# A gated scan followed by a conditioned GRU: direct products of x in the first steps, steps laced into the last chunk, and a first gate in blocks

## The chip, the cores and the metric

The kernel runs on one core of a Trainium2 chip. The core has a matrix engine (PE, with its weight loads shown apart as PEld), a vector engine (DVE), an activation engine (ACT), a general engine (POOL) and a queue engine (SP); each works through its own instructions in order and they wait for each other by semaphores. Transfers are issued from a queue (mostly SP's) and run beside the engines. The metric is the device time of one execution in microseconds (us); lower is better. A profiled execution leaves a record of every instruction, from which the views in this document are taken.

## What is computed

Two layers over x of shape (64 batches, 128 tokens, 512 features), all in 32-bit floats. Layer 0 is a gated linear recurrence that can be done by scans; layer 1 is a GRU whose steps follow each other. Cut to what matters:

```
# layer 0, on x; h0 = cond (64 x 512)
f, i  = sigmoid(x W_f^T + b_f), sigmoid(x W_i^T + b_i)
fn,in = f / (f + i + eps), i / (f + i + eps)
new   = in * (x W_h^T + b_h)
L     = cumsum(log(fn + eps))                 # over tokens
hid   = cumsum(exp(L[-1] - L[t-1]) * new) + exp(L) * h0
x     = x + hid
# layer 1, on the new x; v = cond C + b for each of the gates r, z, h
for t in range(128):                          # h starts at zero
    z  = sigmoid(x_t W_z + h U_z + v_z)
    r  = sigmoid(x_t W_r + h U_r + v_r)
    hh = tanh(x_t W + (r * h) U + v_h)
    h  = (1 - z) * h + z * hh
    out_t = x_t + h
```

## The kernel before

**Layer 0.** The batches go in 16 groups `g` of 4 (`GB`), that is 512 columns of (token, batch). x is loaded with tokens on the partitions, in four blocks of 128 columns per group, and transposed on PE (`x_transposed`, through the helper `transposed`, whose matmuls are L144 and whose copy out of PSUM is L145). The features go in four chunks `c` of 128. For each chunk `chunk_products` makes three gates on PE (`gate`, L181: four 128x512 products each), with the sigmoids of the first two on ACT (L222, L226). Then DVE does the chunk: the sum of both gates (L243), its reciprocal (L244), two products (L258, L261), with ACT adding eps between (L260), then `chunk_new` (L268, a scan L269), `chunk_retained` (a scan backwards L276, a product L281) and `chunk_initial` (a scan L286). POOL works beside the next chunk's reciprocal: the start values (L248), `sums` (L215) and `add_hidden` (L197), which adds x and stores the new x to a DRAM tile `x2d`. `tie` adds an ordering wait, so that these POOL instructions begin after L243. In group 0 the weights of layer 0 have to be transposed too (`w0_transposed`), and behind group 0 `conditioning` computes v on PE (L318).

**Layer 1.** The batches form two streams of 32, so that one stream's products run while the other waits for its sigmoid. In `Stream.step`, a step is: on PE 16 products of h for the gates r and z (L348, g, 256 columns), on ACT the sigmoid (L540), on DVE r times h (L542) and its transpose (L543), on PE 16 products for the candidate (128 columns), on ACT tanh (L570), on DVE the update (L574, L580) and the transpose of the new h (L587). The sum that PE adds to lies in PSUM (`g0` and `g1`, one for each stream) and begins with a share that ACT copies there (`put_share`, L517). A product with zeros comes once before the first share in each.

The share of x is made for two steps at a time by Winograd's form of Strassen's scheme: `queue_pair` puts 7 block products into a list, as 14 units of 4 matmuls (192 columns); they need `s4`, four sums of x on POOL (`gather`, L461 to L464, after an ACT copy L454), and are read out by additions on DVE (L482) and POOL (L485). `fill(n)` issues n units, 7 in each step, between the two products of h, where PE would wait for the sigmoid. The additions are issued in the steps behind (`read`). v is stored as its first half and the difference of its halves, as the additions need it.

**The passage.** Stream 0 needs batches 0 to 31 only, so its gathers 0 and 1 can be made before layer 0 ends. In the last chunk (g = 15, c = 3) the order is written out by hand: `chunk_norm`, gather 1, all of pair 0 and read out, step 0 with pair 1 in it, `chunk_new`, step 1 with `chunk_retained` inside, `chunk_initial`; then the last new x for the first 16 tokens and stream 1's gather 0, its pair 0, read out, and the loop over t from `LEAD` = 2, which alternates stream 0's step t and stream 1's step t - 2. Stream 0's steps 126 and 127 and the end of stream 1 have too few units left to fill; stream 1's steps 126 and 127 are alone, and there `idle_products` multiplies zeros.

`pin` keeps instructions in the program's order on their engine.

Of the kernel before, what the change touches and what calls it, by code (L numbers as in the profile page):

```python
# [14 lines left out]
P = 128  # L15
# [3 lines left out]
def kernel(  # L19
# [72 lines left out]
    def load_x(g, tb, tag="x", bufs=2, queue=nc.sync):  # L92
        rows = work.tile([P, D], F32, tag=tag, bufs=bufs, name=f"x_{g}_{tb}")
        queue.dma_start(
            rows,
            x[g * GB : (g + 1) * GB, tb * TB : (tb + 1) * TB, :].rearrange("b t d -> t b d"),
        )
        x_rows[g, tb] = rows

    load_w_rows(0, 0)  # L100
    for tb in range(K):
        load_x(0, tb, tag="h", bufs=5, queue=(nc.sync, nc.scalar)[tb % 2])
    bias0 = const.tile([3 * K, P], F32, name="bias0")
    for n, v in enumerate((b_f, b_i, b_h)):
        nc.sync.dma_start(bias0[n * K : (n + 1) * K, :], v.rearrange("(c p) -> c p", p=P))
# [63 lines left out]
    w0_transposed(0, 0)  # L169
    for tb in range(K):  # L170
        x_transposed(0, tb, copy=(nc.vector.tensor_copy, nc.scalar.copy)[tb % 2])
# [3 lines left out]
    transposed(biasT, bias0, n=3 * K, m=1)  # L175

    def gate(g, c, n):
        p = psum.tile([P, NT], F32, tag=f"p{n}", name=f"p{n}_{g}_{c}")
        for k in range(K):
            pin(  # L180
                nc.tensor.matmul(  # L181
                    p,
                    lhsT=W0[:, c, n, k, :],
                    rhs=xT[g][:, k, :],
                    start=(k == 0),
                    stop=(k == K - 1),
                )
            )
# [28 lines left out]
    def chunk_products(g, c):  # L217
# [5 lines left out]
        if g == 0 and c == 0:  # L223
            w0_transposed(c, 1)
        p = gate(g, c, 1)
        pin(nc.scalar.activation(ib, p, AF.Sigmoid, bias=biasT[:, 0, K + c : K + c + 1]))  # L226
        if g == 0 and c == 0:
            w0_transposed(c, 2)
            transposed(condT, cond_sb, n=B)
        if g == 0 and c + 1 < K:  # L230
            for n in range(3):
                w0_transposed(c + 1, n)
# [3 lines left out]
        return gate(g, c, 2)  # L236

    def chunk_norm(g, c):
# [14 lines left out]
        if g > 0 or c > 0:  # L253
            before = (g, c - 1) if c else (g - 1, K - 1)
            beside += [sums(*before), add_hidden(*before)]
        for instruction in beside:
            tie(instruction, total)
        pin(nc.vector.tensor_tensor(f, f, h, ALU.mult))  # L258
        fb = by_batch(f)
        pin(nc.scalar.activation(fb, fb, AF.Copy, bias=EPS))  # L260
        return pin(nc.vector.tensor_tensor(i, i, h, ALU.mult))  # L261
# [39 lines left out]
    def conditioning():  # L301
# [27 lines left out]
        for s in range(2):  # L329
            v = const.tile([P, 2, 3, HP], F32, name=f"v{s}")  # L330
            halves, bias_ = (t.rearrange("p g (n e) -> p n g e", n=2) for t in (ps[s], bias1))
            pin(nc.vector.tensor_tensor(v, halves, bias_, ALU.add))
            pin(nc.vector.tensor_tensor(v[:, 1], v[:, 1], v[:, 0], ALU.subtract))
            vs.append(v)
# [56 lines left out]
    def fill(n):  # L391
        for _ in range(n):
            if to_fill:
                unit, reads = to_fill.pop(0)
                unit()
                to_read.extend(reads)
# [12 lines left out]
    class Stream:  # L409
        def __init__(self, s):  # L410
            self.s = s
            self.v = vs[s]
            self.batches = slice(s * SB, (s + 1) * SB)
            self.h = None
# [4 lines left out]
            self.hT = zeros  # L419
# [28 lines left out]
        def gather(self, n):  # L448

# [11 lines left out]
            first_sum = pin(nc.gpsimd.tensor_tensor(s1, a21, a22, ALU.add))  # L461
            pin(nc.gpsimd.tensor_tensor(s2, s1, a11, ALU.subtract))
            pin(nc.gpsimd.tensor_tensor(s3, a11, a21, ALU.subtract))
            pin(nc.gpsimd.tensor_tensor(s4_, a12, s2, ALU.subtract))  # L464
            return first_sum
# [53 lines left out]
        def step(self, t, n_fill=7, n_idle=0, between=None):  # L519
# [4 lines left out]
            xz = self.xz[t // 2 % 2][:, t % 2]  # L524
# [8 lines left out]
            if t > 0:  # L533
# [13 lines left out]
            else:  # L547
                matmuls(g, lambda k: hT_, [w_s[:, 0]], stop=False)
                pin(nc.scalar.activation(rz, xz[:, RZ], AF.Sigmoid))
            fill(n_fill)  # L550
            idle_products(n_idle)
# [167 lines left out]
```

## Time and profile before

| | |
|---|---|
| three runs, median (lowest to highest) | 1995.42 us (1995.08 to 1996.5) |
| the profiled execution: its own time | 1994.23 us |
| its span, first to last instruction | 1992.5 us |
| mean granted TensorE clock | 0.996 |
| PE busy | 1962.2 us, 98% |
| PE weight loads | 1502.6 us, 75% |
| DVE busy | 1367.5 us, 69% |
| POOL busy | 756.0 us, 38% |
| ACT busy | 483.6 us, 24% |
| chain that ended last | PE 66%, DVE 32%, issue 1%, ACT 1% |

How to read it: 98% busy for PE is an average over stages with different limits, and the ends of matmuls are modelled, so a busy PE is not PE at its peak. What a change in one stage is worth is read in that stage. The chain of waits is followed back from the last instruction: at each step to what released it, or to the instruction before it on its engine. In a group row such as "PE g L348 x64" the count is of records; each fp32 matmul leaves two, so x64 is 32 matmuls. Times inside the span are us from its start.

### The profile page before, as it was taken

How to read it: one execution, taken by the hardware profiler on the slowest of the kernel's cores; microseconds unless marked ns; L12 is line 12 of the kernel's file. 1: busy time of each engine (PE TensorE's matmuls, PEld its weight loads, DVE VectorE, ACT ScalarE, POOL GpSimd, SP SyncE). 2: the span in 40 equal slices, each digit the busy share in tenths (PEclk: the TensorE clock that was granted, in tenths of full speed). 3: DMA queues.
4: the chain of work that ended last, by engine and by line, in shares of the span. 5: the costliest groups of instructions: out<-in, count | busy, mean ns of one | idle time of the engine just before them, and what ended most of it. 6: DMA issues, size and time to landing. Idle time of an engine off the chain costs nothing.

```text
span 1992.5 us, 73938 instructions
## 1 busy us (share of the span) xinstructions
PE 1962.2 (98%) x32809; PEld 1502.6 (75%) x32809; DVE 1367.5 (69%) x3017; ACT 483.6 (24%) x1104; POOL 756.0 (38%) x1482
## 2 busy tenths in 40 slices
PE   8999999999999979999999999999999999999997
PEld 4544444444444447777799999999999999999996
DVE  5899999999999975555555555555555555555554
ACT  3222212122122212222222222222222222222222
POOL 1222222222223234444444444444444444444442
PEclk9999999999999989999999999999999999999999
DMA  5411111211111211300220211121120121100111
GB/s 177 170 56 48 48 43 53 63 58 53 43 48 48 71 33 24 62 14 15 43 36 14 40 37 17 35 40 19 35 40 14 19 56 19 20 14 14 19 19 19
DMA packets 228408, 84.66 MB, mean 42 GB/s; under 512 B 205484, under 2 KB 205496, under 8 KB 228088
## 3 DMA queue, kind: packets, MB, share of 16 engines
q1 hardware_dynamic: 227224, 79.34, 16.1%
q8 instruction: 258, 4.23, 0.9%
q10 hardware_dynamic: 864, 0.59, 0.1%
q14 instruction: 62, 0.51, 0.1%
HBM read 46.34 MB, written 33.55 MB: 40 GB/s over the span
## 4 chain that ended last, share of the span: by engine, by line
PE 66%; DVE 32%; issue 1%; ACT 1%; DMA 0%; DVEq 0%; POOL 0%; ACTq 0%; SPq 0%; POOLq 0%
PE g L348 33%; PE m L348 29%; DVE h L244 10%; DVE h L286 4%; DVE i L269 4%; DVE h L276 3%; PE p L181 2%; DVE i L268 2%; DVE i L281 2%; DVE f L258 2%; DVE i L261 2%; DVE h L243 2%; PE tp L144 0%; PE pv L318 0%; DMA x<-in_x_dram 0%
## 5 line engine op out<-in xcount | busy, mean ns | idle before, releaser
L181 PE MATMUL p<-xT,W 128*128 128x512 f32 x1536 | 667.6, 592 | 1.4 <-ACT W L145 0.9
L181 PEld LDWEIGHTS p<-xT,W 128*128 128x128 f32 x1536 | 287.9, 190 | 345.9 <-issue 339.1
L348 PE MATMUL g<-w_s,h 128*32 128x256 f32 x8128 | 503.0, 380 | 2.1 <-DVE h L587 2.1
L348 PEld LDWEIGHTS g<-w_s,h 128*32 128x32 f32 x8128 | 374.7, 110 | 35.3 <-ACT g L517 2.7
L348 PE MATMUL m<-w_t,s 128*32 128x192 f32 x6144 | 345.2, 327 | 0.0
L574 DVE TENSOR_TENSOR h<-h,f 128x128 f32<-128x128 f32 x254 | 74.2, 292 | 343.6 <-ACT h L570 343.6
L589 POOL TENSOR_TENSOR o<-o,h 128x128 f32<-128x128 f32 x254 | 116.3, 458 | 462.4 <-DVE h L580 461.9
L348 PE MATMUL g<-w_s,f 128*32 128x128 f32 x8128 | 285.1, 273 | 4.6 <-DVE f L543 4.5
L348 PEld LDWEIGHTS m<-w_t,s 128*32 128x32 f32 x6144 | 256.3, 110 | 18.2
L348 PEld LDWEIGHTS g<-w_s,f 128*32 128x32 f32 x8128 | 254.2, 110 | 11.3 <-ACT f L540 5.5
L570 ACT ACTIVATE h<-g 128x128 f32<-128x128 f32 x254 | 70.4, 277 | 698.5 <-PE g L348 698.5
L482 DVE TENSOR_TENSOR W<-m,W 128x192 f32<-128x192 f32 x640 | 207.3, 339 | 20.5 <-PE m L348 2.7
L244 DVE RECIPROCAL h<-h 128x517 f32<-128x517 f32 x64 | 217.0, 3391 | 2.2
L248 POOL COPY first<-condT 128x4 f32<-128x4 f32 x64 | 12.1, 190 | 521.0 <-DVE h L243 502.6
L348 PE MATMUL m<-w_x,x 128*32 128x192 f32 x4096 | 200.0, 328 | 6.6 <-ACT x L454 6.6
L542 DVE TENSOR_TENSOR f<-f,h 128x128 f32<-128x128 f32 x254 | 86.3, 340 | 153.3 <-ACT f L540 153.3
L348 PEld LDWEIGHTS m<-w_x,x 128*32 128x32 f32 x4096 | 167.6, 111 | 22.1 <-ACT x L454 6.8
L545 POOL TENSOR_SCALAR f<-f 128x128 f32<-128x128 f32 x254 | 75.5, 297 | 204.8 <-DVE f L542 204.8
L260 ACT ACTIVATE f<-f 128x512 f32<-128x512 f32 x64 | 40.3, 630 | 459.1 <-DVE f L258 459.1
L485 POOL TENSOR_TENSOR W<-W 128x192 f32<-128x192 f32 x256 | 148.0, 600 | 4.8 <-DVE W L482 4.8
L540 ACT ACTIVATE f<-g 128x256 f32<-128x256 f32 x254 | 97.4, 384 | 214.1 <-PE g L348 211.7
L517 ACT COPY g<-W 128x384 f32<-128x384 f32 x254 | 122.7, 483 | 19.2 <-ACT h L570 1.1
(77 smaller groups left out, 1960.3 us busy)
## 6 DMA issues: line engine op xcount, KB each, us to landing
x2d<-x SPq DMA_DIRECT2D x63, 256.0 KB, 2.0
x<-in_x_dram SPq DMA_DIRECT2D x62, 256.0 KB, 3.0
out_dram<-o SPq DMA_DIRECT2D x248, 64.0 KB, 2.0
xw<-x2d SPq DMA_DIRECT2D x60, 256.0 KB, 4.6
w_rows<-in_L_cond_W_f_dram SPq DMA_DIRECT2D x4, 256.0 KB, 3.9
w_rows<-in_L_cond_W_i_dram SPq DMA_DIRECT2D x4, 256.0 KB, 4.0
w_rows<-in_L_cond_W_h_dram SPq DMA_DIRECT2D x4, 256.0 KB, 5.0
w_s<-in_L_cond_U_r_dram SPq DMA_DIRECT2D x1, 1024.0 KB, 5.8
```

The costliest lines, as they stand in the source:

```text
L181: nc.tensor.matmul(p, lhsT=W0[:, c, n, k, :], rhs=xT[g][:, k, :], start=(k == 0), stop=(k == K - 1),)
L244: pin(nc.vector.reciprocal(h, h))
L269: pin(nc.vector.tensor_tensor_scan(i, i, f, 0.0, ALU.add, ALU.mult))
L286: pin(nc.vector.tensor_tensor_scan(h, fs[c % 2], first, 0.0, ALU.mult, ALU.add))
L348: nc.tensor.matmul(p[q * SB : (q + 1) * SB], lhsT=lhsT(k), rhs=part(wk, q), start=(start and k == 0), stop=(stop and k == len(w) - 1), ski ...
L482: return lambda: pin(nc.vector.tensor_tensor(dst, p, other, ALU.add))
L485: return lambda: pin(nc.gpsimd.tensor_tensor(dst, a, b_, ALU.add))
L517: pin(nc.scalar.copy(self.g, self.xz[t // 2 % 2][:, t % 2]))
L540: pin(nc.scalar.activation(rz, g[:, RZ], AF.Sigmoid))
L542: pin(nc.vector.tensor_tensor(rh, r, h_, ALU.mult))
L545: pin(nc.gpsimd.tensor_scalar(r, z, -1.0, 1.0, ALU.mult, ALU.add))
L589: pin(nc.gpsimd.tensor_tensor(o, o, h, ALU.add))
```

## The change

Six steps (0 to 3 of stream 0, 0 and 1 of stream 1) no longer get their share of x from the pairs. ACT copies v whole into the PSUM place (`put_v`), and PE adds the products of x onto it directly, 16 matmuls of 384 columns (`x_products`). The pairs 0 and 1 of stream 0 and 0 of stream 1, and so their additions, are gone. Stream 0 uses both PSUM places at its start, g0 for step 0 and g1 for step 1. Step 0 now stands before the last chunk's `chunk_norm`, step 1 inside it (between the reciprocal and the products with it on DVE in part), step 2 around `chunk_retained`. Gather 0 of stream 0 is made one group earlier, and the four sums of its gather 1 go one by one to the POOL work of four chunks (`spare`). At the end the last pair of stream 1 is queued earlier, and from t = 125 on four units fill a step instead of seven; zeros fill in where no units are left.

In group 0 the first gate is computed in four blocks of 128 columns, each after its block of x, all x blocks come on SP's queue and the biases on ACT's, and each weight's transposes stand one gate ahead of its use, instead of all three behind the second gate.

```
@@ loads
-    def load_x(g, tb, tag="x", bufs=2, queue=nc.sync):
+    def load_x(g, tb, tag="x", bufs=2):
...
-        load_x(0, tb, tag="h", bufs=5, queue=(nc.sync, nc.scalar)[tb % 2])
+        load_x(0, tb, tag="h", bufs=5)
...
-        nc.sync.dma_start(bias0[n * K : (n + 1) * K, :], v.rearrange("(c p) -> c p", p=P))
+        nc.scalar.dma_start(bias0[n * K : (n + 1) * K, :], v.rearrange("(c p) -> c p", p=P))
@@ gate
-    w0_transposed(0, 0)
-    for tb in range(K):
-        x_transposed(0, tb, copy=(nc.vector.tensor_copy, nc.scalar.copy)[tb % 2])
...
-    transposed(biasT, bias0, n=3 * K, m=1)
...
+        blocks = [slice(0, NT)]
+        if (g, c, n) == (0, 0, 0):
+            copies = (nc.vector.tensor_copy, nc.scalar.copy)
+            blocks = [slice(tb * P, (tb + 1) * P) for tb in range(K)]
+            w0_transposed(0, 0)
+            for tb in range(2):
+                x_transposed(0, tb, copy=copies[tb % 2])
+        for tb, tokens in enumerate(blocks):
+            for k in range(K):
+                pin(nc.tensor.matmul(p[:, tokens], lhsT=W0[:, c, n, k, :],
+                    rhs=xT[g][:, k, tokens], start=(k == 0), stop=(k == K - 1)))
+            if len(blocks) > 1 and tb + 2 < K:
+                x_transposed(0, tb + 2, copy=copies[tb % 2])
+            elif len(blocks) > 1 and tb + 2 == K:
+                transposed(biasT, bias0, n=3 * K, m=1)
+                w0_transposed(0, 1)
@@ chunk_products (group 0)
         if g == 0 and c == 0:
-            w0_transposed(c, 1)
+            w0_transposed(0, 2)
+        elif g == 0 and c + 1 < K:
+            w0_transposed(c + 1, 0)
...
-            w0_transposed(c, 2)
             transposed(condT, cond_sb, n=B)
-        if g == 0 and c + 1 < K:
-            for n in range(3):
-                w0_transposed(c + 1, n)
+            w0_transposed(1, 0)
+        elif g == 0 and c + 1 < K:
+            w0_transposed(c + 1, 1)
...
+        if g == 0 and c + 1 < K:
+            for n in range(1 if c == 0 else 2, 3):
+                w0_transposed(c + 1, n)
@@ chunk_norm
+        if spare:
+            beside.append(spare.pop(0)())
...
+        if between:
+            between(normed)
+        else:
+            normed()
@@ Stream
+        def put_v(self):
+            pin(nc.scalar.copy(self.g, self.whole_v))
+
+        def x_products(self, t):
+            x_ = self.x4[t // 4 % 2][:, t % 4]
+            matmuls(self.g, lambda k: x_[:, k * SB : (k + 1) * SB],
+                [w_x[:, k] for k in range(K)], start=False, stop=False)
@@ the passage
-    tie(st0.gather(1), normed)
-    st0.queue_pair(0)
-    fill(2 * 7)
-    read_all()
-    st0.queue_pair(1)
-    st0.step(0, n_fill=2 * 7)
+    g0, g1 = st0.g, st1.g
+    for place in (g0, g1):
+        matmuls(place, lambda _: zeros, [w_s[:, 0]], stop=False)
+        st0.g = place
+        st0.put_v()
+        st0.x_products(0 if place is g0 else 1)
+    st0.g = g0
+    st0.step(0, n_fill=0, share=False)
+    st0.put_v()
+    def x_of_step_2():
+        st0.g = g0
+        st0.x_products(2)
+        st0.g = g1
+    def step_1(rest):
+        st0.g = g1
+        st0.step(1, n_fill=0, share=False, filler=x_of_step_2, between=rest)
+        st0.g = g0
+    chunk_norm(g, c, between=step_1)
+    st1.put_v()
     chunk_new(g, c, p)
     st0.queue_pair(2)
-    st0.step(1, between=lambda: chunk_retained(g, c))
+    fill(7)
+    st0.step(2, share=False, between=lambda: chunk_retained(g, c))
+    st0.put_v()
+    st0.x_products(3)
     chunk_initial(g, c)
...
-    later = to_fill[:]
-    to_fill.clear()
-    st1.queue_pair(0)
-    fill(2 * 7)
-    read_all()
-    to_fill.extend(later)
+    st1.x_products(0)
     for t in range(LEAD, S + LEAD):
-        if t < S:
-            st0.step(t)
+        near_end = t >= S - 3
+        n_fill = 4 if near_end else 7
+        if t == LEAD + 1:
+            st0.step(t, filler=lambda: st1.x_products(1))
+        elif LEAD < t < S:
+            st0.step(t, n_fill, idle=(0 if to_fill else 4, 0))
...
+        if t == S - 3:
+            st, ahead = st1, S - 2
-        st1.step(t - LEAD, n_idle=0 if t < S else 3)
+        lone = t >= S - 1
+        st1.step(t - LEAD, n_fill, idle=(0 if to_fill else 4, 3 * lone), share=t >= LEAD + 1)
+        if t == LEAD:
+            st1.put_v()
```

On the engines' own lists of instructions the change moves nothing between the second group and the last chunk but the gathers, and nothing in the loop between stream 0's step 4 and its step 124.

## What I expected, and why

> **What bounds the kernel now.** I first cut the span at the places where the chain of waits changes character and asked for the busy time of each engine in each stretch: the first group of batches, the other fifteen groups, the passage into the recurrence, the steady recurrence, and its end.
>
> ```profile
> 0.00:76.92 76.92, 70.80 (x460) 38.30 (x461) 46.25 (x46) 20.72 (x36) 11.37 (x22) 1.00 0.58 201
> 76.92:717.45 640.53, 639.12 (x1743) 295.19 (x1741) 616.20 (x540) 135.44 (x236) 177.84 (x181) 1.00 0.17 54
> 717.45:767.48 50.03, 37.31 (x788) 26.21 (x792) 29.00 (x71) 8.61 (x22) 23.18 (x42) 0.86 0.12 28
> 767.48:1947.48 1180.00, 1180.00 (x29053) 1114.45 (x29049) 658.31 (x2299) 309.89 (x786) 531.26 (x1208) 1.00 0.15 27
> 1947.48:1992.50 45.02, 34.93 (x785) 28.43 (x775) 17.77 (x63) 8.94 (x24) 12.36 (x29) 0.96 0.13 20
> ```
>
> Columns: stretch, length, then busy us of PE, PE weight load, DVE, ACT, POOL, the granted TensorE clock, DMA share, GB/s. The second and fourth stretch have no room in them (DVE 96% and PE 100% busy). The change touches almost only the other three, 172 us in which PE is idle for 6, 13 and 10 us. The chain of waits shows why. In the first stretch:
>
> ```profile
> 1.20 5.12 DMA x<-in_x_dram
> ...
> 15.96 3.71 PE p L181 x8
> ...
> 22.96 10.32 PE p L181 x24
> ...
> 35.66 10.32 PE p L181 x24
> ```
>
> PE carries it, but between runs of gates (L181) it stops for transposes whose copies on ACT come late: 3.3 us (19.67 to 22.96), 2.4 (33.28 to 35.66), and likewise 1.3 before and 3.3 after. In the passage:
>
> ```profile
> 743.02 7.20 PE m L348 x112
> ...
> 762.01 2.60 PE g L348 x64
> 764.62 2.27 PE m L348 x56
> 766.89 2.60 PE g L348 x64
> ```
>
> The steady beat of 4.87 us (2.60 for the two products with h, 2.27 for 28 products of x) begins only after stream 1 has been gathered (ACT L454, to 742.97) and its first pair worked off, 56 products in 7.20 us where two beats of 2.27 would be 4.54. At the end:
>
> ```profile
> 1955.59 2.84 PE g L348 x64
> ...
> 1959.72 2.81 PE g L348 x64
> ...
> 1976.46 3.33 PE g L348 x32
> ```
>
> Steps without products to fill them still take 4.13 us (1955.59 to 1959.72), filled ones 4.87, and one product with h takes 3.33 us where the next, at 1983.78, takes 1.97. The clock in these slow runs:
>
> ```profile
> 743.00:747.80 4.80, 4.78 (x60) 2.96 (x64) 0.71 (x2) 0.00 (x0) 4.20 (x6) 0.50 0.02 5
> 1976.40:1979.80 3.40, 3.34 (x36) 2.24 (x40) 0.00 (x0) 0.00 (x0) 0.10 (x1) 0.56 0.00 0
> ```
>
> The granted clock was 0.50 and 0.56 there, after PE had been idle for 6.6 us (736.4 to 743.0) and for half of 6.4 us (1970.0 to 1976.4).
>
> **Part 1, the first group.** Bytes: the DMA windows of 1 us show 299, 381, 277 and 369 GB/s from 2.0 us on, about 330 KB a us. In one queue the first weight (262 KB) then ends near 2.8, x block 0 near 3.6, block 1 near 4.4, block 3 near 6.0, where before block 0 ended at 6.32, sharing with two loads on ACT's queue. PE ends the first weight's transposes at 4.91, so the data no longer decide. From there: 8 cold transposes at 3.88/16 = 0.24 us: 6.85. First quarter gate, cold: 3.44/4 x 2 = 1.72: 8.57. Then I take the full clock (before, the gate at 10.91 ran at it after 4.5 us of work): transposes of four 0.44 (the chain's row at 59.56), quarter gate 0.86. Block 2, quarter, block 3, quarter, bias 0.15, weight 1, quarter, weight 2: 4 x 0.44 + 0.15 + 3 x 0.86 = 4.5, so 13.1; the second gate at 13.2 instead of 15.96, gain 2.75. The copies (DVE 0.69, ACT 0.58) each lie beside a quarter gate or a transpose.
>
> From there to the gate at 76.11 that releases DVE's steady work, PE has 13 gates x 3.44 = 44.7, nine weight transposes and four of x at 0.44 = 5.7, cond 0.46, the conditioning products 5.6: 56.5 us, against 60.15 before. With each weight transposed one gate ahead of its use the difference, 3.65, is the bubbles; I leave 0.4 for handovers. DVE does not take over: its chunks are 10.76 us, and from 17.7 (first sigmoid pair) they would stand ready at 28.4, 40.8, 52.9 for inputs that PE gives at 30.1, 42.2, 54.3. The conditioning weights are loaded once the last transpose has freed their buffer, at 46.7 instead of 47.96; 3.1 MB at the 400 GB/s seen there end near 56, and PE wants them at 57.4. That cover is 1.4 us. SP now issues the two x loads (0.64 us each) where the three biases stood (1.10 together), so the second weight is issued at about the same 3.8 and lands some 4 us later, wanted at 11.2; the biases, now first on ACT, delay the 1.28 us table load by nothing that PE sees. Gain 2.75 + 3.65 - 0.4 = 6.0. Ends: 2.5 (x not before 6.3, cold until 10.9, half the bubbles stay: 15.15 for the second gate, 0.8 + 1.7) and 6.6.
>
> The Trainium skill ("DMA: Bandwidth & Descriptors", section "Issuing engines are not separate DMA queues") says that copies issued by different engines run on the same 16 DMA engines and interleave, so one queue or two gives the same total. If all four blocks then still ended together near 6.3, this term would be 1.4 us smaller, 4.6; the bound at 2.5 already holds that case.
>
> **Part 2, the passage.** Six steps take products of x directly: 16 products of 384 columns each. Four such (the zeros row, 754.92 to 755.57) are 0.65, so 2.60 a step, 5.20 for two steps, against 4.54 for a pair's 56. Three pairs: 2.0 us more for PE. What it buys is order. PE's last gate ends at 713.1. Zeros 0.65, copy of v 0.55 (ACT 0.48, 0.07 of handover), x of step 0 2.60, zeros 0.65, second copy 0.55: 718.2. ACT is in order, so step 0's sigmoid stands behind that second copy: sigmoid and tanh to 718.95, DVE product and transpose to 719.6. Behind these two on DVE waits the last chunk's L243, which was at 717.45: 2.15 us late. L243 and reciprocal: 723.6. POOL (0.19 + 1.28 + 1.52 from 720.25) and ACT's window copy (0.24), which stands before step 1's sigmoid, end at 723.55; sigmoid 723.95; step 1's two DVE operations and the output transpose 724.85; L258 and L261 726.2. PE meanwhile does x of step 1, the h product, x of step 2 (to 725.15), the last h product 726.05. Tanh 726.6, three DVE operations 727.55, L268 and L269 729.65 (before: 729.1). So DVE has done step 1 inside the chunk at a price of 0.55. Then 28 products and h product on PE to 730.05, sigmoid, three DVE operations, one read, 731.7; L276 and L281 733.6; step 2's tail 734.85; L286 736.1 (before 741.2, where eight more reads and waits for half-speed products lay between). POOL 0.7, copy 0.25, gather 0.63: stream 1's first product at 737.85 instead of 743.02. The reads of two pairs (14 DVE additions of 0.34 and the POOL ones) are what has left this chain.
>
> From there PE is solid: x 2.60, 28 products 2.27, h 1.73, x 2.60, 2.27, 2.60, 2.27, 0.87 = 17.2, so stream 0's step 4 begins at 755.05. Before it began at 767.59. PE never rests for longer than 1.1 us in this, so I give it the full clock. Gain 12.5; I take 12.4. Ends: stream 1's gather no earlier than before and half speed behind it (743.0 + 17.2 + 2.7, the 2.7 being 7.20 - 4.54: 762.9, gain 4.7) and PE without its last 1.1 us of rest (13.5).
>
> The Trainium skill ("TensorE: Matmul & The Clock Gate", section "Part 1: The HAM clock gate") has the clock halve after an idle window of about 3.4 us and return after a busy one. The rows above agree for the 6.6 us, but at 1976.4 the clock fell without any gap over 1.6 us, so PE's two rests of 0.55 and one of 1.1 are not proved safe. By the rule the term stays 12.4; by that row it could lose the 2.7 of the lower end.
>
> **Part 3, the end.** From the h product of stream 0's step 125 (1947.48) to the span's end before: 45.0. After: products are spread 4 units (16) a step, 1.28 us, into gaps where the unfilled cadence leaves PE 1.3 us idle: five steps of 4.13 = 20.65 (before 22.86, because three of them were filled with 28). Step 125 of stream 1 to step 126: 6.1 as before. The 12 zero products now behind its last product (0.97) fit in the 2.63 until h is ready, and if they hold the clock, step 126 is like 127 was, 3.31 + 2.63 = 5.94 instead of 7.32. From step 127's start to the end 8.72 as before. Sum 20.65 + 6.1 + 5.94 + 8.72 = 41.4, gain 3.6. Ends 1.5 (clock still falls, and the first read on DVE costs 0.15 a step) and 3.8.
>
> **Nothing for the rest.** The sums of the second gather go to POOL one in each of four chunks, behind 2.99 us of POOL work that begins with the 3.39 us reciprocal, 0.46 each: hidden under DVE's L244 and L258. Run together beside scans, as the first gather is, four such stretched a chunk from 10.76 to 11.15; so 0 to 0.4. That first gather and its four window loads move a group earlier at the same 0.39; on SP only x loads needed a group later stand behind them. The two copies of v on ACT (about 0.3 each by the 128x256 row's 0.39) fall where ACT is idle. In the steady stretch each engine keeps its order.
>
> **Sum.** 6.0 + 12.4 + 3.6 = 22.0. The profiled execution took 1994.23 (span 1992.5 and 1.7 around it), so 1972.2; it lies 1.2 under the median 1995.42, so the forecast for the median is 1973.4.
>
> **Rivals.** (a) The serial start of steps 0 and 1 holds the last chunk back, a wait in place of the one removed: DVE order puts it before L243. Against it, only 2.15 us are lost there. If stream 1's gather is not earlier at all, the passage gains 7.5 and the time is 1978.3. (b) The first group's gain is hidden: the conditioning weights or the x blocks land as before. At 2.5 instead of 6.0 the time is 1976.9, at 0 1979.4. (c) Slower: 21 products (an odd number) leave the order, so every later product takes the other half of its PSUM bank, and in the steady 1180 us PE might wait for a read. There are 242 beats; from 0.09 us a beat (22.0/242) the whole gain is gone, at 0.12 the time is 1973.4 + 29 = 2002. Against it: a pair has 7 products, so both halves already alternate, and PE has no wait in that stretch. (d) The clock falls in the passage and at the end: 2.7 + 1.4, 1977.5.
>
> **How the numbers follow.** Forecast as worked out (within 3 us) 0.55, (a) 0.15, (b) 0.13, (d) 0.10, (c) 0.03, the rest 0.04 for a stall that I do not see. The range goes from all upper ends (6.6 + 13.5 + 3.8 = 23.9, 1971.5, less 1 for the measure) to where (a) and (b)'s 2.5 meet, 1981.8: 1970.5 to 1982. About 0.2% (4 us) is what a measurement can tell from no change. Faster by more 0.95, within 0.02, slower 0.03.
>
> **What would show it.** In the profile after: the second gate near 13.2; DVE's steady chunks from about 71; L243 of the last chunk 2 us behind its predecessor; stream 1's first product 20 us after that L243's place (737.85 - 717.45) and stream 0's step 4 at 37.6 after it; granted clock near 1.0 in the passage and at the end; from stream 0's step 125 to the end 41.4; the beat still 4.87. A beat above 4.9, or a passage of over 44 us, would make the prediction wrong.

## The result, and the profile after

| | before | after |
|---|---|---|
| median of four runs each, side by side (lowest to highest) | 1995.25 us (1994.65 to 1996.5) | 1975.32 us (1974.34 to 1976.27) |
| ratio of times, 95% interval | | 0.9899 (0.9882 to 0.9916) |
| the profiled execution: own time, span | 1994.23, 1992.5 us | 1976.27, 1974.4 us |
| mean granted clock | 0.996 | 1.0 |

The change takes 19.9 us off by the medians; I had forecast 1973.4, and it came out at 1975.3. On another chip the same two kernels differ by 18.0 (`changed_again` below: 1992.56 and 1974.59). The profiled execution happens to be the slowest of its four. Cut at the same five places as before (stretch, length, then busy us of PE, PE weight load, DVE, ACT, POOL, the granted clock, DMA share, GB/s), the trace after is:

```profile
0.00:73.47 73.47, 68.64 (x484) 38.85 (x485) 46.24 (x45) 21.35 (x38) 11.35 (x22) 1.00 0.63 214
73.47:713.85 640.38, 639.14 (x1695) 293.57 (x1693) 616.06 (x540) 136.44 (x238) 179.51 (x185) 1.00 0.17 53
713.85:752.10 38.25, 35.71 (x708) 21.95 (x704) 22.62 (x51) 8.35 (x22) 17.76 (x32) 1.00 0.15 37
752.10:1932.10 1180.00, 1179.05 (x29006) 1029.45 (x29001) 657.88 (x2298) 309.52 (x786) 530.33 (x1207) 1.00 0.15 27
1932.10:1974.40 42.30, 36.32 (x859) 28.67 (x851) 17.73 (x64) 8.95 (x24) 13.41 (x31) 1.00 0.14 22
```

The steady stretches are as they were; the first group is 3.45 us shorter, the passage about 12 (50.03 to 38.25, at cuts that differ a little), the end about 3. Cut exactly at the prediction's own places, the two profiled executions compare so (the last two boundaries are products with h of stream 0's step 4 and step 125):

| part (us) | before | after | gain | predicted |
|---|---|---|---|---|
| 1: start to the sum of group 1's first chunk (L243, now L260) | 76.92 | 73.47 | 3.45 | 6.0 |
| the other groups, to the end of chunk (15, 2) | 640.53 | 640.38 | 0.15 | 0 |
| 2: from there to step 4 | 50.14 | 38.07 | 12.07 | 12.4 |
| steady recurrence, to step 125 | 1179.89 | 1181.12 | -1.23 | 0 |
| 3: from there to the end | 45.02 | 41.36 | 3.66 | 3.6 |

The steady stretch lost 1.23 us in this one execution: the waits of PE in it hold two of 0.5 us without a releaser. In a second profile of the same kernel (`changed_again` below) there are none, and the stretch, taken between the sigmoids of the same steps, is 1179.75 us long against 1181.29, so I count that as chance.

So Part 1 is where the sum was off. Its chain of waits (start, length, what):

```profile
1.21 3.77 DMA x<-in_x_dram
...
5.03 0.79 PE tp L144 x4
...
12.48 3.44 PE p L186 x8
...
47.42 10.21 DMA cw<-in_L_cond_C_dram
...
57.77 2.88 PE pv L344 x129
60.65 1.41 issue
62.06 2.85 PE pv L344 x127
...
65.53 0.53 issue
66.06 6.61 PE p L186 x15
```

The second gate (L186) begins at 12.48, where in the profile of before its like began at 15.96: 3.48 us won, more than the 2.75 predicted (how much of that belongs to that one execution is shown behind the next three runs). Then nothing more is won to the end of the group: 60.99 us from there to the sum, against 60.96. The chain names why. PE's products for v (pv, L344) wait for the conditioning weights (cw), whose load takes 10.21 us from its issue and lands at 57.63. And in the middle of these products and again behind them PE stands still for 1.41 and 0.53 us with no releaser that the profile could name. The passage:

```profile
734.04 0.63 ACT x L487
...
734.71 2.79 PE g L376 x32
737.50 2.27 PE m L376 x56
739.77 4.31 PE g L376 x64
744.08 2.27 PE m L376 x56
746.36 2.60 PE g L376 x64
```

Stream 1 is gathered (L487) at 734.04 instead of 742.34, its first 16 products of x take 2.79 us where the pair took 7.20, and the beat of 2.27 and 2.60 begins at once. PE has no rest from 734.71 on. The end:

```profile
1936.44 2.76 PE g L376 x64
1939.19 1.30 PE m L376 x32
1940.49 2.77 PE g L376 x64
...
1959.89 1.93 PE g L376 x32
```

The 4 units a step (1.30 us) lie in what was rest, the steps come every 4.07 us (1940.49 to 1944.56, and so on), and the first lone product with h takes 1.93 us where it took 3.33.

### The profile page after: what moved, and what is told of

The parts are those of the page before. It is cut to its first block, busy times and chain, and to the rows that moved or that the text cites. A ratio compares the mean times of both kernels' runs of the same rounds, so it can differ in the third digit from the quotient of the medians.

```text
span 1974.4 us, 73723 instructions
## 1 busy us (share of the span) xinstructions
PE 1958.9 (99%) x32729; PEld 1412.5 (72%) x32729; DVE 1360.5 (69%) x2996; ACT 484.6 (25%) x1108; POOL 752.4 (38%) x1476
## 4 chain that ended last, share of the span: by engine, by line
PE 70%; DVE 27%; issue 1%; DMA 1%; ACT 0%; DVEq 0%; SPq 0%; POOL 0%; ACTq 0%; POOLq 0%
PE g L376 34%; PE m L376 29%; DVE h L261 9%; PE p L186 6%; DVE h L312 3%; DVE i L295 3%; DVE h L302 3%; DVE i L294 2%; DVE i L307 2%; DVE f L279 2%; DVE i L282 2%; DVE h L260 2%; DMA cw<-in_L_cond_C_dram 1%; PE tp L144 1%; DMA x<-in_x_dram 0%
## 5 line engine op out<-in xcount | busy, mean ns | idle before, releaser
L186 PE MATMUL p<-xT,W 128*128 128x512 f32 (+1 forms) x1560 | 669.4, 586 | 0.7 <-issue 0.5
L186 PEld LDWEIGHTS p<-xT,W 128*128 128x128 f32 x1560 | 290.0, 190 | 341.7 <-issue 336.4
L376 PE MATMUL g<-w_s,h 128*32 128x256 f32 x8128 | 527.8, 379 | 1.1 <-DVE h L638 1.1
L376 PEld LDWEIGHTS g<-w_s,h 128*32 128x32 f32 x8128 | 336.4, 110 | 98.1 <-ACT g L554 1.8
L376 PE MATMUL m<-w_t,s 128*32 128x192 f32 x6000 | 376.7, 326 | 0.0
L376 PE MATMUL g<-w_s,f 128*32 128x128 f32 x8128 | 311.5, 273 | 2.5 <-DVE f L597 1.5
L376 PEld LDWEIGHTS m<-w_t,s 128*32 128x32 f32 x6000 | 263.6, 110 | 21.5 <-issue 0.4
L376 PEld LDWEIGHTS g<-w_s,f 128*32 128x32 f32 x8128 | 270.1, 110 | 10.8 <-issue 4.2
L623 ACT ACTIVATE h<-g 128x128 f32<-128x128 f32 x256 | 70.9, 277 | 697.7 <-PE g L376 697.7
L519 DVE TENSOR_TENSOR W<-m,W 128x192 f32<-128x192 f32 x625 | 202.3, 339 | 20.3 <-PE m L376 3.2
L376 PE MATMUL m<-w_x,x 128*32 128x192 f32 x4000 | 206.8, 326 | 0.0
L265 POOL COPY first<-condT 128x4 f32<-128x4 f32 x64 | 12.1, 190 | 508.6 <-DVE h L260 494.0
L376 PE MATMUL m<-w_x,s 128*32 128x192 f32 x2000 | 125.8, 326 | 0.0
```

The source lines that it names most:

```text
L186: nc.tensor.matmul(p[:, tokens], lhsT=W0[:, c, n, k, :], rhs=xT[g][:, k, tokens], start=(k == 0), stop=(k == K - 1),)
L376: nc.tensor.matmul(p[q * SB : (q + 1) * SB], lhsT=lhsT(k), rhs=part(wk, q), start=(start and k == 0), stop=(stop and k == len(w) - 1), ski ...
L519: return lambda: pin(nc.vector.tensor_tensor(dst, p, other, ALU.add))
L623: pin(nc.scalar.activation(hh, g[:, 2], AF.Tanh))
```

## The experiments

Twelve runs in three groups; those of a group ran on one chip, beside runs of the kernel before on it. The median of the kernel before differed, and lay below the 1995.25 us it had beside the result: 1992.9 us in the first group (21 runs, 1990.79 to 1994.77), 1992.56 in the second (9), 1993.6 in the third (15).

### The three parts alone

`start_only` is the kernel before with all hunks of group 0 (loads, `gate`, `chunk_products`), among them:

```
-        load_x(0, tb, tag="h", bufs=5, queue=(nc.sync, nc.scalar)[tb % 2])
+        load_x(0, tb, tag="h", bufs=5)
...
+            blocks = [slice(tb * P, (tb + 1) * P) for tb in range(K)]
```

> The kernel before with the changes in group 0 alone (first gate in blocks, x on one queue, transposes one gate ahead). Theory: the parts add and each shows in its own stretch; here DVE's first L243 of group 1 comes at about 73.5 instead of 76.9, since PE has to wait for the conditioning weights behind group 0: 3.5 us less than before. Rival, the sum as predicted: 70.7, 6.0 us less. Rival, hidden: 0 to 1 less.

1989.91 us (1988.72 to 1991.75), ratio 0.9985 (0.9976 to 0.9994): 3.0 us less. The sum of group 1 comes at 72.88, and the same places stall: PE waits for the weights, then 1.10 us and 0.26 us without a releaser. The 6.0 of the prediction is out: the fastest of the eleven executions lies 4.2 below the median of before. So the shortfall belongs to this part.

`passage_only` is the changed kernel with the start and the end of the kernel before:

```
-        near_end = t >= S - 3
-        n_fill = 4 if near_end else 7
...
-        load_x(0, tb, tag="h", bufs=5)
+        load_x(0, tb, tag="h", bufs=5, queue=(nc.sync, nc.scalar)[tb % 2])
```

> The kernel before with the passage alone (direct products, steps laced into the last chunk, gathers moved); start and end as before. Theory: from the end of the next to last chunk (717.45 before) to stream 0's step 4 some 38.2 us instead of 50.1, 11.9 us less than before in all. Rival (a serial start holds the last chunk back once the first group is not earlier): 7 to 8 us less.

1980.08 us (1979.54 to 1985.14), ratio 0.9941 (0.9929 to 0.9954): 12.8 us less. Stream 1's gather begins 20.39 us after the end of chunk (15, 2)'s scan (before: 24.89). The clock is 1.00 in the whole passage.

`end_only` is the kernel before with the new end:

```
+        near_end = t >= S - 3
+        n_fill = 4 if near_end else 7
...
-            st0.step(t)
+            st0.step(t, n_fill, idle=(0 if to_fill else 4, 0))
...
+        if t == S - 3:
+            st, ahead = st1, S - 2
```

> The kernel before with the end alone (four units a step from step 125 on, zeros behind the lone products). Theory: 41.4 us from step 125 to the end instead of 45.0, 3.6 us less than before. Rival (the clock falls all the same): 2.2 us less.

1990.65 us (1988.6 to 1994.82), ratio 0.9992 (0.9983 to 1.0): 2.25 us less by the medians, with an interval that reaches to nothing. The spread follows the mean granted clock of each run: 1988.6 to 1989.7 at 0.997, 1994.8 at 0.994. In the profiled run the stretch from step 125's sigmoid to the end takes 39.84 us, against 42.94 in the profile of before: 3.1 less there. The clock falls in this run only in the passage, which is still the old one; that the spread comes from there in the other runs too is likely, but they have no profile.

The three add up to 18.1, what the whole gains in the next group (18.0); beside the result it was 19.9.

These variants also show that the one profile of before on which the prediction was built was slow in two places. With the old start, the second gate begins at 15.96 us in it; in `passage_only`, `end_only` and `before_zeros` (a later run) the same instruction stands at:

```profile
14.43 3.71 PE p L181 x8
13.98 3.71 PE p L181 x8
13.58 3.71 PE p L181 x8
```

With the new start it lies between 12.33 and 13.07 in nine profiles. The same holds for the old end: the first lone step takes 7.25 us in the profile of before, with a fall of the clock in it, and 5.86 to 5.87 in `passage_only`, `start_only` and `before_zeros`, without one; from step 125's sigmoid to the end it is 42.94 us there, 41.54 to 41.84 in these three, and 39.22 after the change. So 1.5 to 2.4 us of the 3.48 at the start, and 1.1 to 1.4 us of Part 3's 3.66, lie in that execution and not in the change. Against the other profiles the new end gains 2.3 to 2.6, and `end_only`'s median gain of 2.25 is nearer to its rival's 2.2 than to the 3.6, though not for the rival's reason: in its profile the clock held there (5.87).

### Why Part 1 fell short

`cw_free` is the changed kernel with the conditioning weights in a buffer that is free from the start, so that their load does not wait for the last weight transpose:

```
-        cw = load_weights("cw", (C_r, C_z, C_h), "wa")
+        cw = load_weights("cw", (C_r, C_z, C_h), "wc")
```

> The changed kernel with the conditioning weights loaded into the buffer that the differences of weights take only from group 3 on, so that they need not wait for the last transposes. Theory (that load is what took back the first group's gain, and PE's stalls without a visible releaser, 1.41 and 0.53 us beside it, come from the same full transfer engines): L243 of group 1 at 71.0 instead of 73.5, 2.5 us less than the changed kernel (1975.3), 1972.8. Rival (the stalls are PE's own, whatever is loaded): only the wait of 0.6 goes, 1974.7. Rival (loads of the next weights collide in its place): no change.

1973.26 us (1972.84 to 1974.0), ratio 0.9901 (0.9885 to 0.9916). The sum of group 1 comes at 70.47, as against the 70.9 of the prediction (76.92 - 6.0) and the 73.47 with the shared buffer. `changed_again`, the changed kernel once more in the next group, shows that the stalls of the changed kernel were no accident of one execution:

> The changed kernel itself, beside its variants on the same chip. Every theory expects about 20 us less than before. If the late transfers are the cause of the stalls in the conditioning products, these come again: g1c0's sum near 73.5 and 1 to 2.5 us of waits for the conditioning weights or without a releaser; if they were an accident of one execution, g1c0 stands near 71.0.

1974.59 us (1974.36 to 1974.75), ratio 0.991 (0.9895 to 0.9925). The sum comes at 73.04, with a wait of 0.46 us for the weights and 1.01 and 0.53 us of unnamed rest. The same stretch in the chain of `early_cw` below, which has the free buffer:

```profile
53.98 3.44 PE p L186 x8
57.42 5.42 PE pv L346 x256
62.84 13.50 PE p L186 x31
```

The products for v go through in one piece of 5.42 us, with no wait and no rest before or behind them. What the unnamed rests are is only hinted at. In the list of transfers, an instruction block (queue, kind: packets, MB, share of the engines) moves at 58 to 59 in the changed kernel:

```profile
q8 instruction: 1, 0.02, 10.8%
```

and at 54 to 56 in `early_cw`, although the data transfers fill 97.9% of that window:

```profile
q1 hardware_dynamic: 375, 0.74, 97.9%
q8 instruction: 1, 0.02, 3.0%
```

That fits a PE that runs out of instructions at 60.65 because the next block came 4 us later, but the list does not say whose instructions the block holds, and no run shows it. What held the block was not tried either; as the engines were as full in `early_cw`, a full DMA alone is not it.

### One queue or two for the first x

The base is `early_cw`, the best version so far, which has no cover behind the start in which a loss could vanish. `early_cw_again` ran it in the third group, and `early_cw_2q` gives x blocks 1 and 3 back to ACT's queue and the biases to SP's:

```
-        load_x(0, tb, tag="h", bufs=5)
+        load_x(0, tb, tag="h", bufs=5, queue=(nc.sync, nc.scalar)[tb % 2])
...
-        nc.scalar.dma_start(bias0[...], ...)
+        nc.sync.dma_start(bias0[...], ...)
```

> The version with both single edits again, as the base for the next two on this chip: about 21.7 us below before.

> That version with the first x blocks 1 and 3 back on ACT's queue and the biases on SP's, as before the change. Prediction's theory: in one queue block 0 lands first, in two it shares with its neighbours, so the first transposes of x wait until about 6.2 and the second gate comes at about 1.4 us later; with no cover left behind it, the time rises by 1.2 to 1.4. Rival, the rule of one set of DMA engines behind all queues (the Trainium skill, DMA: Bandwidth & Descriptors, Issuing engines are not separate DMA queues): the total is the same and only shares move, so under 0.4.

1971.14 us (1970.56 to 1971.72) for the base, ratio 0.9889 (0.9875 to 0.9902); 1973.9 (1972.01 to 1975.63), ratio 0.9899 (0.9884 to 0.9915), with two queues: 2.76 more. The chain of the base:

```profile
1.20 3.73 DMA x<-in_x_dram
...
4.97 1.13 PE tp L144 x4
...
6.87 1.16 PE p L186 x8
...
12.77 3.44 PE p L186 x8
```

and with two queues:

```profile
1.20 4.64 DMA x<-in_x_dram
...
5.89 1.97 PE tp L144 x8
7.85 2.01 PE p L186 x8
...
15.26 3.44 PE p L186 x8
```

Block 0 lands 0.91 us later, but the second gate comes 2.49 later. The rest is speed: PE was idle from 4.9 to 5.89, and its next products ran at the cold rate for longer, 2.01 us for a quarter gate that took 1.16. The windows of the profile read a granted clock of 1.00 in both, but in the record of clock changes that each trace keeps, the first entry, the rise to full, stands at 6.30 us in the base and at 11.12 with two queues. The first group's sum comes 2.78 later (73.70 against 70.92), and one lone step at the end, in which the clock falls, takes 6.77 us instead of 5.87.

This profile is of the longest of the four runs, though, and they lie in two pairs: 1972.01 and 1972.41, 0.9 and 1.3 above the base's median, and 1975.38 and 1975.63, 4.2 and 4.5 above it. The other profiles with x on two queues show what can differ. PE's first transpose of x begins at 6.37 us in `before`, 6.18 in `passage_only`, 4.94 in `end_only` and 4.89 in `before_zeros`; with one queue it is 4.70 to 5.05 in nine profiles. The clock rises at 10.76, 5.26, 4.90 and 5.84 us in these four. So block 0 is late in some executions and not in others, and the same wait costs clock in `before` and none in `passage_only`, where the rise came ahead of it.

So the rival (under 0.4) fell, as all four runs lie above the base's four; my price of 1.2 to 1.4 fits the first pair, and the 2.76 of the medians lies between two kinds of executions, of which only one has a profile. The Trainium skill ("DMA: Bandwidth & Descriptors", section "Issuing engines are not separate DMA queues") says that copies of all queues run on the same 16 engines and interleave; from that I had taken an equal total. Up to 6.0 us two queues moved 229 GB/s, one queue 186 (224 to 241 and 185 to 199 in all profiles), so the total was if anything better with two. What decided in this execution was when block 0 was complete, and what PE did meanwhile.

### How much of the passage is clock

`before_zeros` keeps the order of the kernel before, and gives PE products with zeros in the two long waits of the passage, so that its clock does not fall:

```
-    fill(2 * 7)
+    fill(12)
+    for _ in range(9):
+        matmuls(st0.g, lambda _: zeros, [w_s[:, 0]], stop=False)
+    fill(2)
...
+    for _ in range(9):
+        matmuls(st1.g, lambda _: zeros, [w_s[:, 0]], stop=False)
     st1.queue_pair(0)
```

> The kernel before, with products with zeros (36 of 384 columns, about 5.9 us at full clock) in each of the passage's two waits of PE, which end at 723.6 and 743.0; the order of the work stays. It parts the passage's 11.9 us into clock and order. Prediction's theory: order is most of it; held at full clock, the pair after the gather gives back 7.20 - 4.54 = 2.7 us, and the pair after 723.6 at most as much again, so the time falls by 2.7 to 5.3. Rival: the clock is most of it, the time falls by 8 or more. Third: the gathers come at the same place and the DVE and POOL additions set the end of both stretches, so the time falls by under 1.

1988.25 us (1986.82 to 1991.14), ratio 0.9973 (0.9964 to 0.9982): 5.35 less, at the upper end of what the theory gave. In its chain:

```profile
738.98 0.63 ACT x L454
739.65 4.76 PE m L348 x112
```

The pair takes 4.76 us, not 7.20, and the gather comes 23.52 us after the scan's end, not 24.89. From the scan's end to the sigmoid of step 4 it is 48.29 us here, 52.12 before and 40.0 after. So of the 12.1 us that the passage gains by that measure, holding the clock in the old order is worth 3.8 and the new order the other 8.3. (The old passage takes 51.83 us in `end_only` and 53.33 in `start_only`, so the clock's share is 3.5 to 5.0 by execution.) The granted clock of the kernel before, by windows:

```profile
720.20:723.60 3.40, 0.00 (x0) 0.02 (x1) 3.23 (x6) 1.38 (x3) 1.01 (x2) 0.58 0.21 77
723.60:727.00 3.40, 3.39 (x36) 1.93 (x40) 2.21 (x8) 1.07 (x3) 2.82 (x7) 0.50 0.35 82
```

PE has stopped at 717.2 and does nothing in the first of these windows (0.00), in which the clock halves; it stays at 0.50 through the second, in which PE is busy all the time. The two profiled executions differ by 7.1 us: besides these 3.8, this one's first group ended at 75.03, 1.9 us earlier with the same instructions, and its first lone step at the end kept the clock (5.87 us instead of 7.25). Neither comes from the zeros. Which of this stands behind the other 1.5 of the medians' 5.35 is not shown.

### Are the zeros at the end needed

`no_zeros` leaves out the 12 products with zeros behind each lone product:

```
-        st1.step(t - LEAD, n_fill, idle=(0 if to_fill else 4, 3 * lone), share=t >= LEAD + 1)
+        st1.step(t - LEAD, n_fill, idle=(0 if to_fill else 4, 0), share=t >= LEAD + 1)
```

> The changed kernel without the 12 products with zeros behind each lone product at the end. Prediction's theory: the zeros keep the clock up, so without them one product with h falls to half speed and the end is 1.4 us longer each time. Rival, after the first runs: where PE rests in the end's last steps, the clock falls or not by where its window lies, so some executions lose 1.4 us and others nothing, and the median is 0 to 1.4 us above the changed kernel's. Third: nothing at all, the lone steps stay at 5.87 each.

1977.91 us (1976.75 to 1980.23), ratio 0.9928 (0.9916 to 0.9941): 3.3 more than the changed kernel on this chip, and all five runs lie above its four. All three expectations were too small. All five runs of `no_zeros` have a mean clock of 0.998 or 0.999, the changed kernel's four 1.0, so the clock fell in each. In each trace the changes of the clock lie whole multiples of 3.41 us apart, so I count PE's work in windows on that grid, first in `no_zeros`:

```profile
1953.07:1956.48 3.41, 1.30 (x31) 0.74 (x24) 1.33 (x6) 0.38 (x1) 0.99 (x3) 1.00 0.16 24
1956.20:1959.60 3.40, 1.91 (x32) 1.48 (x32) 1.28 (x6) 0.76 (x2) 1.27 (x4) 0.54 0.00 0
```

and in the changed kernel (`changed_again`):

```profile
1951.44:1954.85 3.41, 2.44 (x56) 1.60 (x46) 1.14 (x4) 0.66 (x2) 0.87 (x2) 1.00 0.16 26
1954.85:1958.27 3.42, 2.36 (x64) 1.97 (x68) 1.89 (x7) 0.76 (x2) 1.76 (x4) 1.00 0.00 0
```

The last window ahead of the fall at the end of the kernel before, and the emptiest one of `early` (below) near its end, in which the clock held:

```profile
1973.42:1976.84 3.42, 1.46 (x40) 1.18 (x44) 2.22 (x8) 0.76 (x2) 2.31 (x5) 1.00 0.02 5
1952.37:1955.78 3.41, 1.71 (x53) 1.35 (x48) 1.04 (x4) 0.44 (x2) 1.78 (x4) 1.00 0.13 19
```

Without the zeros the clock falls at 1956.48 and both products of a step are slow: 3.61 us for the one with h (1.93), 1.94 for the candidate's (1.11), together 2.5; the step takes 8.38 instead of 5.87. I had counted only one slow product. Another 0.66 lies in the step before it (5.24 instead of 4.58), which the last experiment explains. The Trainium skill ("TensorE: Matmul & The Clock Gate", section "Part 1: The HAM clock gate") ties the fall to an idle window of about 3.4 us; here it fell behind a window with 1.30 us of work and after no gap over 2.1 us. In this case's traces it fell behind windows with 1.24 to 1.46 us of work, that is 0.36 to 0.43 of 3.41, in five places (and behind emptier ones), and held behind 1.65 to 1.71, 0.48 to 0.50, in three; one with 1.40 (`end_only`) held too, so the border lies near there and is not sharp. Nor do the zeros make it safe: the profiled runs of `cw_free` and `early_cw_2q`, which have them, show a lone step of 6.76 and 6.77 us, behind windows with 1.35 and 1.39 us of work.

### Step 0 behind the last chunk's first sum

In the changed kernel step 0's DVE work stands ahead of the last chunk's first sum and holds it back by 2.1 us. `early` puts it behind, and makes both copies of v before the products of x:

```
     for place in (g0, g1):
         matmuls(place, lambda _: zeros, [w_s[:, 0]], stop=False)
         st0.g = place
         st0.put_v()
+    for place in (g0, g1):
+        st0.g = place
         st0.x_products(0 if place is g0 else 1)
...
-    st0.step(0, n_fill=0, share=False)
-    st0.put_v()
...
-    chunk_norm(g, c, between=step_1)
+    chunk_norm(g, c, between=step_1, first_step=step_0)
```

where `first_step` is called in `chunk_norm` between the sum (L260) and the reciprocal.

> The changed kernel with step 0's DVE operations behind the last chunk's first sum instead of ahead of it, and both copies of v ahead of both sets of products of x. Theory: the 2.1 us by which the sum came late were spent waiting for step 0's sigmoid, so the sum comes at 1 to 2 us earlier, the reciprocal and step 1 about 1.5 us earlier, and the time falls by 1.5. Rival: PE's products of x set the passage, so the sum is earlier but stream 1's gather is not, and the time stays.

1973.51 us (1973.05 to 1973.84), ratio 0.9904 (0.9891 to 0.9918): 1.1 less than the changed kernel on this chip. DVE in the changed kernel, `changed_again` (start, us, engine, line, operation, idle before):

```profile
715.00 0.29 DVE L628 TENSOR_TENSOR h<-h,f 128x128 f32<-128x128 f32 x1 [1.35 <-ACT h L623]
...
715.56 0.88 DVE L260 SCALAR_TENSOR_TENSOR h<-f,i 128x517 f32<-128x517 f32 x1
716.47 3.39 DVE L261 RECIPROCAL h<-h 128x517 f32<-128x517 f32 x1
```

and in `early`:

```profile
713.55 0.67 DVE L260 SCALAR_TENSOR_TENSOR h<-f,i 128x517 f32<-128x517 f32 x1
...
715.02 3.35 DVE L263 RECIPROCAL h<-h 128x517 f32<-128x517 f32 x1
```

DVE's wait of 1.35 us for ACT's tanh of step 0 (L623) is gone, as the sum fills it; the reciprocal comes 1.38 us after the end of chunk (15, 2), where it came 3.02 after it. Stream 1's gather comes 19.04 us after that end, against 20.23: 1.2 of it arrives. The rival (PE's products of x set the passage) is out. The two hunks of this edit were not run apart.

`early_cw` has both edits.

> Both single edits together: the conditioning weights in a buffer that is free from the start, and step 0 behind the last chunk's first sum. If both theories hold, their gains add, as they lie in stretches 640 us apart: 2 to 3 us from the first, 1.5 from the second, 3.5 to 4.5 below the changed kernel on the same chip. If early gains nothing, 2 to 3.

1970.89 us (1970.56 to 1971.1), ratio 0.9891 (0.9877 to 0.9904): 3.7 below the changed kernel. The two gains add.

### A store in front of a sigmoid

`early_cw_sp` issues stream 0's last store from SP alone; two of its four transfers were ACT's:

```
-                queue = nc.scalar if t == S - 1 and q % 2 else nc.sync
+                queue = nc.scalar if self.s == 1 and t == S - 1 and q % 2 else nc.sync
```

> That version with stream 0's last store issued by SP alone, where ACT issued two of its four transfers. Theory: ACT's two issues stand ahead of stream 1's sigmoid of step 126 and hold it by 0.3 to 0.9 us (the step took 4.58 to 5.2 us where the ones before it took 4.07), so the time falls by 0.3 to 0.5. Rival: the sigmoid waits for PE or for POOL's addition anyway, and nothing changes.

1970.1 us (1970.03 to 1970.3), ratio 0.9884 (0.987 to 0.9897): 1.04 less than its base on the same chip, twice what was expected. ACT in the base (`early_cw_again`):

```profile
1949.74 1.61 ACTq L662 DMA_DIRECT2D out_dram<-o  x2
1951.47 0.38 ACT L596 ACTIVATE f<-g 128x256 f32<-128x256 f32 x1 [2.48 <-DMA out_dram<-o]
```

and without the store:

```profile
1949.87 0.38 ACT L596 ACTIVATE f<-g 128x256 f32<-128x256 f32 x1 [1.50 <-PE g L378]
```

In brackets stands the idle time before and what ended it. The sigmoid of stream 1's step 126 stood behind two issues that took 1.61 us together; without them it waits for PE's product alone, and the step takes 4.11 us like those before it, instead of 5.10. This is the best version run: 4.7 us below the changed kernel by the two same-chip steps (3.70 and 1.04).

## Why the prediction was right, and where it was off

The forecast of 1973.4 lay 1.9 below the median, and the median inside its range. The mechanism held in all three parts but for one wait, and the sum also owes something to luck: it was worked out from one profile of before in which the clock rose late and fell at the end, and the kernel before took about as long beside the result. On the chip of `changed_again`, where before took 1992.56, the gain was 18.0 of the 22.0. Step by step:

- **Part 1, to the second gate: the place right, the gain in part luck.** Predicted 13.2, measured 12.48. The data came later than I had it (x block 0 at 4.98, not near 3.6), but PE's first weight ended near the same time, and the clock rose earlier (at 5.32 us): the first quarter gate took 1.16 us, not the cold 1.72. Against the other three profiles of the old start it gains 1.1 to 1.95, where 2.75 was predicted.
- **Part 1, from there to the sum: the step that failed.** I wrote that the conditioning weights would end near 56 and that "that cover is 1.4 us". I let them start at 46.7 and took 400 GB/s; the last of three was issued at 47.42, the windows of 2 us from 48 to 56 show 324, 385, 355 and 372 GB/s, and they landed at 57.63. PE waited 0.62 for them, and then came 1.41 and 0.53 of rest, for which the trace of before has no row. Together 2.56, most of the 3.3 us (3.65 less 0.4) that this stretch was to give and did not. With the weights in their own buffer they are there (70.47 against the 70.9 forecast). From the second gate to the sum it is then 58.15 us in `early_cw_again` and I had said 57.7, so the bubbles were counted rightly.
- **Part 2: right in mechanism, size and places.** The last chunk's sum came 2.1 us late (2.15 said), stream 1's first product 20.86 after the scan's end (20.4), step 4 at 38.07 (37.6), and from stream 1's first product on PE was solid for 17.21 us (17.2). Rival (a) is answered by `early`: the delay of 2.1 was real, and 1.2 of it went on to the gather. What I did not separate is that 3.8 of the 12 are the clock's; the half-speed pair was in the sum, but the earlier fall (720.7) stands in it only as "waits for half-speed products", without a price.
- **Part 3: right in sum (3.66 for 3.6), and that is partly luck.** Five steps at about 4.1, as said; the step that I put at "6.1 as before" took 6.37 and held the store of the last experiment. The term of 1.38 (5.94 instead of 7.32) takes away a fall of the clock that the three other profiles with the old end do not have; against them the new end gains 2.3 to 2.6. What the zeros are worth in the new end is another number: without them two products are slow and the time is 3.3 longer, 2.5 of it in these two.
- **Nothing for the rest.** The groups between changed by 0.15, the beat stayed at 4.87. Rival (c), a longer beat, did not come; rival (b) came in part (3.45, between its 2.5 and the 6.0), rival (d) not at all in these runs, though a version with the same end showed it.

## What to carry to other kernels

Where a gain moves a stage's end forward, the loads behind that stage must move with it: a cover of about a microsecond, worked out from a transfer rate, is none, and the issue of the transfers belongs in the sum. A wait on PE is paid twice when it lets the clock fall, so price the products behind it too, both of a step and not one. And on an engine that works in order, the issue of a store is work like any other: in front of an operation on the chain it costs what of its time that operation would not have waited anyway, here 1.0 of 1.61 us. And a single profile of the kernel before is a sample: a term that takes away a late clock there is worth that only as often as the clock is late.

## What the runs showed of the hardware

- The start and the end of the same instructions differ from run to run: group 1's first sum came at 76.92, 75.79, 75.03 and 74.93 in four profiles of the old start, and the first lone step of the old end took 7.25 us in one profile and 5.86 to 5.87 in three others.
- After PE stops, the clock fell 3.5 us later in one place (717.2; 0.58 as the mean of the window from 720.2 puts the fall near 720.7) and 4.8 in another (736.4; 0.59 from 740.6 on puts it near 741.2), and without a long gap in a third (`no_zeros`). In each trace the changes lie whole multiples of 3.41 us apart (in `before` at 720.73, 727.56, 741.21, 748.04, 1976.84 and 1980.25). Whether a short rest costs anything depends on where it lies on that grid, not on its length alone.
- At the start the same holds for the rise: in `early_cw_2q` the window from 4.29 to 7.71 us, with PE's wait of 0.98 in it and 2.44 us of work, was followed by another at the cold rate; in all fourteen profiles the window ahead of the rise was busy for 0.9 of its length or more.
- Two issues of a store on ACT took between 0.86 us (`before`) and 1.74 us (`no_zeros`) for the same transfers.
